# Pools that wait tile by tile on two stacks, and the ternary weights of layer 1 prepared inside layer 0

## The chip, the core and the metric

The kernel runs on one core of a Trainium2 chip. A core has five engines with queues of their own: TensorE (PE for its matmuls, PEld for its weight loads), VectorE (DVE), ScalarE (ACT), GpSimd (POOL) and SyncE (SP), which here only issues DMA transfers. Each engine works through its queue in order. Data lies in SBUF, 128 partitions wide, and the results of matmuls in PSUM, 8 banks of 2 KB per partition. The metric is the time of one execution in microseconds of device time; lower is better.

## The reference: four layers of cross-attention and feed-forward

x has 16 tiles of 128 tokens by 256 features. Each of four layers adds a cross-attention to the context of the same tile and then a feed-forward, each on a layer norm of x:

```
x = x + L0_xattn(norm(x), ctx)   # 16 heads, int8-rounded weights and activations
x = x + L0_ffn(norm(x))          # causal self-attention (16 query heads, rotary), then 8 experts
x = x + L1_xattn(norm(x), ctx, mask)
x = x + L1_ffn(norm(x))          # ternary weights
x = x + L2_xattn(norm(x), ctx)   # 16 heads
x = x + L2_ffn(norm(x))          # 64 low-rank routes, the best 4
x = x + L3_xattn(norm(x), ctx)   # every query against all 2048 context rows
x = x + L3_ffn(norm(x))          # 8 experts and 2 shared
```

The change touches the weights of L1_ffn, which the reference rounds so:

```
def weight_quant(w):
    scale = 1.0 / jnp.clip(jnp.mean(jnp.abs(w)), EPS, None)
    return jnp.clip(jnp.round(w * scale), -1.0, 1.0) / scale
gate = bit_linear(x, w_gate); up = bit_linear(x, w_up)
activated = subln(up * jnp.square(jax.nn.relu(gate)), subln_weight)
return bit_linear(activated, w_down)
```

Three matrices of 256 x 1024 are divided by their mean absolute value, rounded and cut to -1, 0, 1. Only layer 3 looks across tiles, and it does so through the context alone; layers 0 to 2 of a tile need nothing of another tile.

## The kernel before: three stages of pools and interleaved steps

The program has three stages: layer 0 (`l0`), layers 1 and 2 with the keys and values of layer 3 (`middle`), and layer 3 (`l3`). In each, the work on a tile is cut into generators that yield between steps. `side_by_side` (line 122) holds a table `starts` of step numbers, starts generators at their step and advances all running ones by one piece a step. In layer 0 tile t starts its cross-attention (`l0_xattn`) at step 4t, the keys of the self-attention (`l0_keys`) at 4t+8, its four groups of heads (`l0_group`) at 4t+11 to 4t+14, its experts (`l0_moe`) at 4t+17. In `middle` it starts `l1_xattn` at 4t, `l3_keys` at 4t+2, `l1_ffn` at 4t+3, `l2_xattn` at 4t+7, `l2_ffn` at 4t+16, and `l3_values` starts once at step 4.

The steps are only the order in which the program is written. The framework's scheduler then sets the order of each engine's queue, taking instructions as they get ready, the earlier written first, and adds the semaphores. In `l3` the order is fixed by hand (`manual_schedule`, line 1142).

A tile of SBUF or PSUM comes from a pool. A pool has a number of buffers for each tag and lies on a stack: a pool opened after another has been closed takes over its bytes. As written before, the first use of a new pool waits until the pools whose bytes it takes have been released as a whole. All pools lie on one stack (left). The streams have two pools each, one for tiles and one, `_s`, for small columns (`stream`, line 116).

The joint between the stages: `run` (line 1182) opens pool w0 with all weights of layer 0, closes it, opens w3 (weights of layer 3's attention and its keys `kst` and values `v_int`), and inside it `middle` opens w1 (weights of layers 1 and 2), the PSUM pool with tags e=1, w=3, x=2, av=1, f=1 bank, and calls `l1_ffn_weights` (line 612). That loads gate, up and down into a pool l1r (8 KB per partition each), sums their absolute values (line 622), adds the sums over the partitions with one matmul (line 624), and rounds: two passes on VectorE (lines 631, 632) and one on ScalarE, which writes bf16 (line 633). `load`, `rows` and `cols` (lines 91 to 113) each issue one DMA on SP. Then come the loads of `l2_xattn_weights`, `l2_ffn_weights` and `l3_kv_weights`, and with the first step those of `l1_xattn` for context and mask (lines 583, 585). Layer 0's PSUM pool has tags x, av, aq, a, as, ap with one bank each, and m with two; `l1_xattn` and `l1_ffn` work through tag e, `l3_keys` and `l3_values` and `l2_ffn` through tag f, `l1_ffn`'s gate and up and `l2_ffn`'s vecs through tag w.

Layer 3's first steps (lines 1146 to 1155): norm (965), transpose (971), projection (980), quantisation (987), transpose of q (1004), scores (916), then the exponentials on ScalarE (938). Each takes a bank from b0 to b6 in turn (`take`, line 904).

Of the kernel before, what the change touches and what calls it, by code (L numbers as in the profile page):

```python
# [4 lines left out]

# [1 line left out]

# [1 line left out]

# [9 lines left out]
F32 = mybir.dt.float32  # L19
BF16 = mybir.dt.bfloat16  # L20
# [5 lines left out]
ALU = mybir.AluOpType  # L26
AX = mybir.AxisListType
PSUM = bass.MemoryType.PSUM

P = 128  # L30
# [10 lines left out]
class Net:  # L41
# [66 lines left out]
    def cols(self, name, tag):  # L108
# [3 lines left out]
        self.nc.sync.dma_start(t, self.i[name].rearrange("(c p) -> p c", p=P))  # L112
        return t

    @contextmanager
    def stream(self, name, bufs=2, small=3, tag=None):

        with (self.tc.tile_pool(name=name, bufs=bufs) as pool,
              self.tc.tile_pool(name=f"{name}_s", bufs=small) as sm):
            yield pool, sm, tag or name  # L120

    def side_by_side(self, starts):
# [26 lines left out]
    @contextmanager  # L149
    def psum(self, **bufs):  # L150

        with self.tc.tile_pool(name="psum", bufs=1, space=PSUM) as self.ps:
            self.bufs = bufs
            yield
            self.ps = None
# [174 lines left out]

    def l0_xattn_weights(self):
        w = {}
        with self.tc.tile_pool(name="l0x_q", bufs=1) as pool:
            w["q"], w["sq"] = self.quant_weight("L0_xattn_wq", pool, "l0q")
            w["p"], w["sp"] = self.quant_weight("L0_xattn_wp", pool, "l0p")
        w["kv"] = self.load("L0_xattn_wkvT", [P, 2, 512], "x2", "(c p) o -> p c o", p=P)
        w["bq"], w["bp"] = self.rows("L0_xattn_bq", "b0"), self.rows("L0_xattn_bp", "b1")
        w["bv"] = self.rows("L0_xattn_bkv", "b2", slice(D, 2 * D))
        w["bk"] = self.cols("L0_xattn_bkv", "bc0")
        return w  # L340
# [102 lines left out]

    def l0_ffn_weights(self, pool):
        nc, w = self.nc, {}
        w["q"] = self.load("L0_ffn_qT", [P, 2, 2048], "wa", "(c p) n -> p c n", p=P)
        w["kv"] = self.load("L0_ffn_kvT", [P, 2, 1024], "wc", "(c p) n -> p c n", p=P)
# [12 lines left out]
        w["ct"], w["st"] = ct, st  # L460
        w["moe"] = self.moe_weights("L0_ffn", 8)
        return w

    def rotated(self, ps, w, j, pool):
# [88 lines left out]
        out = yield from self.moe(hT, w["moe"], 8, 1e-9, pool, 1)  # L553
        nc.vector.tensor_tensor(self.x[t], out, self.x[t], ALU.add)

    @contextmanager
    def l0_weights(self, pool):
        self.tag = "x"
        yield self.l0_xattn_weights(), self.l0_ffn_weights(pool)

    def l0(self):

        with self.tc.tile_pool(name="l0w", bufs=1) as wp, self.psum(x=1, av=1, aq=1, a=1, **{"as": 1}, ap=1, m=2), self.l0_weights(wp) as (wx, wf), (
                self.stream("x", bufs=1, small=2)) as sx, self.stream("a") as sa, self.stream("m", small=2) as sm:
            tiles = {}

            starts = {}
            for t in range(NT):
                starts.setdefault(4 * t, []).append((sx, lambda p, t=t: self.l0_xattn(t, wx, p)))
                starts.setdefault(4 * t + 8, []).append((sa, lambda p, t=t: self.l0_keys(t, wf, tiles, p)))  # L570
                for g in range(4):
                    starts.setdefault(4 * t + 11 + g, []).append(
                        (sa, lambda p, t=t, g=g: self.l0_group(t, g, wf, tiles, p)))
                starts.setdefault(4 * t + 17, []).append((sm, lambda p, t=t: self.l0_moe(t, wf, tiles, p)))
            self.side_by_side(starts)
        self.tag, self.small = None, self.small0


    def l1_xattn(self, t, pool):
# [32 lines left out]
    def l1_ffn_weights(self):  # L612

        nc, W = self.nc, self.W1
        w = {"subln": self.rows("L1_ffn_subln_weight", "subln")}
        with self.tc.tile_pool(name="l1r", bufs=1) as pool:
            raw = [self.load("L1_ffn_gateT", [P, 2, W], "ra", "(c p) n -> p c n", p=P, pool=pool),
                   self.load("L1_ffn_upT", [P, 2, W], "rb", "(c p) n -> p c n", p=P, pool=pool),
                   self.load("L1_ffn_downT", [P, 8, D], "rc", "(c p) n -> p c n", p=P, pool=pool)]
            sums = self.s(3, "wsum")  # L620
            for j, r in enumerate(raw):
                nc.vector.tensor_reduce(sums[:, j:j + 1], r, AX.XY, ALU.add, apply_absolute_value=True)
            ps = self.mm([P, 3], "wtot")
            nc.tensor.matmul(ps, self.ones, sums, start=True, stop=True)
            mean = w["mean"] = self.w.tile([P, 3], F32, name="wmean", tag="wmean")
            nc.vector.tensor_scalar(mean, ps, 1.0 / (W * D), 1e-5, ALU.mult, ALU.max)
            r = self.s(3, "wr")
            nc.vector.reciprocal(r, mean)
            for j, (n, v) in enumerate(zip(("gate", "up", "down"), raw)):
                w[n] = self.w.tile(list(v.shape), BF16, name=f"tern{j}", tag=f"tern{j}")  # L630
                nc.vector.tensor_scalar(v, v, r[:, j:j + 1], 1.0, ALU.mult, ALU.min)
                nc.vector.tensor_scalar(v, v, -1.0, MAGIC, ALU.max, ALU.add)
                nc.scalar.activation(w[n], v, AF.Identity, bias=self.unmagic)
        return w

    def l1_ffn(self, t, w, pool):

# [223 lines left out]

    def middle(self, w3):

        with (self.tc.tile_pool(name="w1", bufs=1) as self.w, self.psum(e=1, w=3, x=2, av=1, f=1)):
            self.tag = "e"
            w1f = self.l1_ffn_weights()
            w2x, w2f, w3k = self.l2_xattn_weights(), self.l2_ffn_weights(), self.l3_kv_weights()
            with (self.stream("f", bufs=1, small=2) as s2f, self.stream("x", bufs=1, small=2) as s2x,
                  self.stream("kv", bufs=1, small=2, tag="f") as s3, self.stream("f1", bufs=1, small=2, tag="e") as s1f,
                  self.stream("x1", bufs=1, small=2, tag="e") as s1x):  # L870
                starts = {}
                for t in range(NT):
                    for step, st, make in ((0, s1x, lambda p, t=t: self.l1_xattn(t, p)),
                                           (3, s1f, lambda p, t=t: self.l1_ffn(t, w1f, p)),
                                           (7, s2x, lambda p, t=t: self.l2_xattn(t, w2x, p)),
                                           (16, s2f, lambda p, t=t: self.l2_ffn(t, w2f, p)),
                                           (2, s3, lambda p, t=t: self.l3_keys(t, w3k, w3, p))):
                        starts.setdefault(4 * t + step, []).append((st, make))
                starts[4].append((s3, lambda p: self.l3_values(w3k, w3, p)))
                self.side_by_side(starts)  # L880
        self.tag, self.small = None, self.small0

    def l3(self, w3, moe_w):
# [10 lines left out]
        NE, IN = 10, 176  # L894
        LAG = 4
        E = mybir.EngineType
        with (tc.tile_pool(name="l3x", bufs=2) as pool, tc.tile_pool(name="l3p", bufs=3) as pp,
              tc.tile_pool(name="l3t", bufs=LAG + 1) as tp, tc.tile_pool(name="l3m", bufs=1) as mp,
              tc.tile_pool(name="l3e", bufs=3) as ep):
            st = {}  # L900

            banks = {f"b{j}": float(j - 7) for j in range(7)}
# [278 lines left out]

    def run(self):
        self.load_x()
        with self.tc.tile_pool(name="w0", bufs=1) as self.w:
            self.l0()
        with self.tc.tile_pool(name="w3", bufs=1) as self.w:
            w3 = self.l3_weights()
            self.middle(w3)
            with self.tc.tile_pool(name="w4", bufs=1) as self.w:
# [72 lines left out]
```

## Time and profile before

| | |
|---|---|
| median of 3 runs | 3008.33 us (3003.62 to 3014.27) |
| the profiled execution's own time | 3011.51 us |
| its span, first to last instruction | 3009.8 us |
| busy in the span | PE 2460.5 (82%), DVE 1956.3 (65%), ACT 1755.0 (58%), POOL 1000.7 (33%), PEld 1556.2 (52%) |
| last addition of layer 0 to x (line 554) | 1154.6 us after the start |
| last addition of layer 2 to x (line 770) | 1862.5 us |
| first exponential of layer 3 (line 938) | 1877.5 us |
| weights loaded by SP around the joint (8960 KB in 24 transfers) | issued 1121.9 to 1169.3 us |

The page cuts the span into 40 slices of 75 us and gives a digit of busy tenths for each; the granted clock of TensorE has a line of its own. Slices 0 to 14 are layer 0, 15 to 24 the middle, the rest layer 3:

```profile
PE   4789999999999875888888885777777777777778
...
ACT  1234444444444332555555541998888888888885
...
PEclk9899999999999887999999997589899898989999
DMA  5000000000000003000000002876666666666673
```

TensorE is at 9 through most of layer 0 and falls to 7 and 5 at its end; it is at 8 in the middle and falls to 5 at that one's end; in layer 3 ScalarE is the busiest. The DMA engines work at the beginning, in slice 15, and through layer 3.

### The profile page before, as it was taken

The page shows a single profiled execution, that of the slowest core. Times are in us where ns is not written, and L with a number is a line of the kernel's source. Part 1 is how long each engine was busy: PE and PEld are TensorE (multiplying, and loading weights), DVE is VectorE, ACT ScalarE, POOL GpSimd, SP SyncE. Part 2 cuts the span into 40 slices and gives each one's busy share as a digit, 9 for nine tenths or more (in the row PEclk, how much of TensorE's full clock was granted, in tenths as well). Part 3 has the DMA queues.
Part 4 walks back from the last instruction along what each step waited for, and adds up shares of the span by engine and source line. Part 5 has one row for each costly group of instructions (what it writes and reads, how often), then busy time and mean ns, then how long its engine had stood idle before and what let it go on. Part 6 is the DMA issues. An engine that isn't in the chain of part 4 may idle for free. (4 is left out here: it accounts for less than half of the span.)

```text
span 3009.8 us, 41685 instructions
## 1 busy us (share of the span) xinstructions
PE 2460.5 (82%) x14066; PEld 1556.2 (52%) x14066; DVE 1956.3 (65%) x5041; ACT 1755.0 (58%) x4636; POOL 1000.7 (33%) x1587
## 2 busy tenths in 40 slices
PE   4789999999999875888888885777777777777778
PEld 2456666666666543456555653344444444444445
DVE  2455666666665434566666653887788787878784
ACT  1234444444444332555555541998888888888885
POOL 2344444444443322555555541111111111112111
PEclk9899999999999887999999997589899898989999
DMA  5000000000000003000000002876666666666673
GB/s 205 1 1 1 1 1 1 1 1 1 1 1 1 1 28 102 6 3 5 5 5 4 3 1 72 154 135 123 124 117 128 121 124 121 126 122 125 118 128 62
DMA packets 559830, 171.38 MB, mean 57 GB/s; under 512 B 538912, under 2 KB 555904, under 8 KB 558848
## 3 DMA queue, kind: packets, MB, share of 16 engines
q1 hardware_dynamic: 559616, 168.72, 27.8%
q8 instruction: 111, 1.82, 0.2%
q14 instruction: 103, 0.84, 0.1%
HBM read 32.37 MB, written 2.10 MB: 11 GB/s over the span
## 5 line engine op out<-in xcount | busy, mean ns | idle before, releaser
L938 ACT ACTIVATE p<-piece,nb,hs 128x512 int16<-128x512 f32 x1024 | 785.2, 791 | 27.4 <-issue 17.0
L922 DVE TENSOR_REDUCE nm<-piece 128x1 f32<-128x512 f32 x1024 | 652.1, 684 | 107.7 <-PE piece L916 99.8
L916 PE MATMUL piece<-kst,qT 128*128 128x512 bf16 x1024 | 366.5, 414 | 200.6 <-DVE ma L1099 89.6
L1100 POOL TENSOR_TENSOR act<-ma,mb 128x176 f32<-128x176 f32 x160 | 89.0, 558 | 765.1 <-DVE ma L1099 764.7
L233 PE MATMUL gu<-w_L_ffn_wgu,mhT 128*128 128x352 f32 x640 | 252.5, 523 | 11.6 <-ACT p L938 8.0
L225 ACT COPY pT<-tp 128x512 f32<-128x512 f32 (+1 forms) x208 | 116.6, 563 | 201.6 <-PE tp L209 200.1
L916 PEld LDWEIGHTS <-qT 128*128 128x128 bf16 x1024 | 77.4, 99 | 297.2 <-issue 168.8
L938 ACT ACTIVATION_READ_ACCUMULATOR p<-piece,nb,hs 128x1 f32 x1024 | 222.2, 217 | 0.0
L259 POOL TENSOR_TENSOR kx<-kT,hmask 128x512 f32<-128x512 f32 x128 | 132.8, 1043 | 190.4 <-PE scores L262 125.4
L264 DVE TENSOR_REDUCE mx<-scores 128x4 f32<-128x512 f32 x128 | 88.2, 689 | 161.3 <-PE scores L262 161.0
L233 PEld LDWEIGHTS gu<-w_L_ffn_wgu,mhT 128*128 128x128 f32 x640 | 122.7, 205 | 131.4 <-ACT p L938 83.5
L950 PEld LDWEIGHTS <-pT 128*128 128x128 f16 x4096 | 144.7, 99 | 82.6 <-issue 68.0
L278 PEld LDWEIGHTS av<-v,pT 128*128 128x128 f32 x1024 | 136.2, 201 | 78.2 <-ACT pT L225 66.6
L233 PE MATMUL gu<-w_L_ffn_wgu,hT 128*128 128x352 f32 x512 | 173.7, 461 | 2.1 <-DVE act L432 1.6
L524 ACT ACTIVATE s<-s,nb,qs 128x128 f32<-128x128 f32 x256 | 123.2, 482 | 87.2 <-DVE nb L522 87.2
L278 PE MATMUL av<-v,pT 128*128 128x17 f32 x1024 | 136.3, 265 | 41.0 <-ACT pT L225 41.0
L269 ACT ACTIVATE p<-scores,mx,qs 128x128 f32<-128x128 f32 x256 | 96.9, 459 | 118.8 <-DVE mx L267 111.0
L950 PE MATMUL av<-v_int,pT 128*128 128x16 bf16 x4096 | 143.7, 171 | 19.6 <-DVE o L1021 19.6
L262 PE MATMUL scores<-kx,qT 128*128 128x512 f32 x256 | 153.0, 682 | 2.3 <-ACT qT L225 1.8
L539 PE MATMUL oproj<-w_L_ffn_oT,oT 128*128 128x256 f32 x512 | 128.9, 396 | 3.7 <-ACT oT L533 3.6
L1119 PE MATMUL moe<-w_L_ffn_wd,aT 128*128 128x256 f32 x448 | 127.7, 434 | 3.6 <-ACT p L938 3.6
L233 PE MATMUL q<-w_L_ffn_qT,hT 128*128 128x512 f32 x256 | 127.9, 600 | 2.1 <-DVE rot L478 2.0
(362 smaller groups left out, 5305.7 us busy)
## 6 DMA issues: line engine op xcount, KB each, us to landing
pT<-p SPq DMA_TRANSPOSE x256, 4.3
w_L_ffn_wgu<-in_L_ffn_wgu SPq DMA_DIRECT2D x1, 3520.0 KB, 11.6
w_L_ffn_wgu<-in_L_ffn_wgu SPq DMA_DIRECT2D x1, 2816.0 KB, 12.7
x<-in_x SPq DMA_DIRECT2D x16, 128.0 KB, 4.5
ctxT<-in_ctxT SPq DMA_DIRECT2D x4, 512.0 KB, 5.2
w_L_ffn_qT<-in_L_ffn_qT SPq DMA_DIRECT2D x1, 2048.0 KB, 7.9
w_L_ffn_oT<-in_L_ffn_oT SPq DMA_DIRECT2D x1, 2048.0 KB, 15.6
ctx<-in_ctx SPq DMA_DIRECT2D x16, 128.0 KB, 2.0
```

The costliest lines, as they stand in the source:

```text
L225: nc.scalar.copy(out[:, j0:j0 + m, :], ps)
L233: self.nc.tensor.matmul(ps, a, b, start=(j == 0), stop=(j == n - 1))
L259: nc.gpsimd.tensor_tensor(kx, kT[oc].unsqueeze(1).to_broadcast([P, 4, P]), self.hmask[:, hs].unsqueeze(2).to_broadcast([P, 4, P]), ALU.mult)
L262: nc.tensor.matmul(ps, qT[:, oc, :], kx, start=True, stop=True)
L278: nc.tensor.matmul(av[:, 4 * g + h, :], pT[:, h, :], v[:, 4 * g + h, :], start=True, stop=True)
L524: nc.scalar.activation(s[:, j, :], s[:, j, :], AF.Exp, bias=nb[:, j:j + 1], scale=qs[:, j:j + 1], accum_out=z[:, j:j + 1])
L539: nc.tensor.matmul(proj, oT[:, j, :], w["o"][:, c, :], start=(c == 0), stop=(c == 15))
L916: nc.tensor.matmul(ps, qTs[t % 2][:, hd, :], kst[q // 2][:, hd // 2, 512 * (q % 2):512 * (q % 2) + 512], start=True, stop=True)
L922: nc.vector.tensor_reduce(st["nm", u][:, q:q + 1], st["s", u, q][0], AX.X, ALU.max, negate=True)
L938: nc.scalar.activation(p[:, 512 * q:512 * q + 512], ps, AF.Exp, bias=nb, scale=st["sq", t][:, hd:hd + 1], accum_out=st["z", t][:, hd, q:q ...
L950: nc.tensor.matmul(st["av", t][:, hd, :], pb[:, c, :], v[:, c, hd * 16:(hd + 1) * 16], start=(c == 0), stop=(c == NT - 1))
L1119: nc.tensor.matmul(ps, st["aT", k][:r, j, :], wd[:r, c, :], start=(c == 0), stop=(c == 13))
```

## The change

Every pool except the two constant ones is opened with `reuse_waits="tile"`: a tile waits for those tiles alone whose bytes it takes over, not for their whole pool. The pools lie on two stacks: on the right layer 0's cross-attention (wx and stream x), later layer 1 (w1, x1, f1), later the experts of layer 3 (w4); on the left the rest. When layer 0's cross-attention has been written to its end, at step 68 of layer 0, a generator `prepare` closes its two pools, opens w1 in their place and runs `l1_ffn_weights` there, in pieces between the steps 68 to 71: load and round one matrix after the other through two raw buffers instead of three, each with its own sum, matmul (in bank x of layer 0), and mean. `middle` opens its streams in another order (x1 and f1 on the right; then w2, kv, x, f on the left). In `l0_ffn_weights` the load of keys and values comes before that of the queries, and the experts' weights have a pool of their own, wm.

```diff
+    def pool(self, name, bufs, side="left"):
+        return self.tc.tile_pool(name=name, bufs=bufs, side=side, reuse_waits="tile")
...
-        with self.tc.tile_pool(name="psum", bufs=1, space=PSUM) as self.ps:
+        with self.tc.tile_pool(name="psum", bufs=1, space=PSUM, reuse_waits="tile") as self.ps:
...
+    def l0(self, late):
+        early = ExitStack()
         self.tag = "x"
+        with self.psum(x=1, av=1, aq=1, a=1, **{"as": 1}, ap=1, m=2):
+            self.w = early.enter_context(self.pool("wx", 1, "right"))
+            wx = self.l0_xattn_weights()
+            sx = early.enter_context(self.stream("x", bufs=1, small=2, side="right"))
+            with (self.pool("wa", 1) as self.w, self.stream("a") as sa, self.pool("wm", 1) as wm,
+                  self.stream("m", small=2) as sm):
+                wf = self.l0_ffn_weights(self.w)
+                self.w = wm
+                wf["moe"] = self.moe_weights("L0_ffn", 8)
+                self.tiles(wx, wf, sx, sa, sm, early, late)
...
+        def prepare(pool):
+            early.close()
+            self.w = late.enter_context(self.pool("w1", 1, "right"))
+            yield from self.l1_ffn_weights()
+        starts.setdefault(4 * NT + 4, []).append((sa, prepare))
+        self.side_by_side(starts)
...
+        with self.pool("l1r", 1, "right") as pool:
+            raw = {n: self.load(f"L1_ffn_{n}T", shape, f"raw{j % 2}", "(c p) n -> p c n", p=P, pool=pool)
+                   for j, (n, shape) in enumerate(shapes.items()) if j < 2}
+            for j, (n, shape) in enumerate(shapes.items()):
+                yield
+                if j == 2:
+                    raw[n] = self.load(f"L1_ffn_{n}T", shape, "raw0", "(c p) n -> p c n", p=P, pool=pool)
+                v, total, r = raw[n], self.s(1, "wsum"), self.s(1, "wr")
+                nc.vector.tensor_reduce(total, v, AX.XY, ALU.add, apply_absolute_value=True)
+                ps = self.bank([P, 1], "x", "wtot")
+                nc.tensor.matmul(ps, self.ones, total, start=True, stop=True)
+                nc.vector.tensor_scalar(mean[:, j:j + 1], ps, 1.0 / (W * D), 1e-5, ALU.mult, ALU.max)
+                nc.vector.reciprocal(r, mean[:, j:j + 1])
+                nc.vector.tensor_scalar(v, v, r, 1.0, ALU.mult, ALU.min)
                 nc.vector.tensor_scalar(v, v, -1.0, MAGIC, ALU.max, ALU.add)
                 nc.scalar.activation(w[n], v, AF.Identity, bias=self.unmagic)
...
+        with (self.psum(e=1, w=3, x=2, av=1, f=1), self.stream("x1", bufs=1, small=2, tag="e", side="right") as s1x,
+              self.stream("f1", bufs=1, small=2, tag="e", side="right") as s1f, self.pool("w2", 1) as self.w,
+              self.stream("kv", bufs=1, small=2, tag="f") as s3, self.stream("x", bufs=1, small=2) as s2x,
+              self.stream("f", bufs=1, small=2) as s2f):
             w2x, w2f, w3k = self.l2_xattn_weights(), self.l2_ffn_weights(), self.l3_kv_weights()
...
     def run(self):
         self.load_x()
+        late = ExitStack()
+        self.l0(late)
+        with self.pool("w3", 1) as self.w:
             w3 = self.l3_weights()
             self.middle(w3)
+            late.close()
+            with self.pool("w4", 1, "right") as self.w:
                 moe_w = self.moe_weights("L3_ffn", 10)
```

The tables of starts are the same but for `prepare`, and the arithmetic on x is the same.

More of the change, by code (lines that the diff above doesn't have):

```diff
@@ L8 @@
-from contextlib import contextmanager
+from contextlib import ExitStack, contextmanager
 import numpy as np
@@ L113, in cols, with stream @@
         return t
+    def pool(self, name, bufs, side="left"):
+        return self.tc.tile_pool(name=name, bufs=bufs, side=side, reuse_waits="tile")
     @contextmanager
-    def stream(self, name, bufs=2, small=3, tag=None):
-        with (self.tc.tile_pool(name=name, bufs=bufs) as pool,
-              self.tc.tile_pool(name=f"{name}_s", bufs=small) as sm):
+    def stream(self, name, bufs=2, small=3, tag=None, side="left"):
+        with (self.pool(name, bufs, side) as pool,
+              self.pool(f"{name}_s", small, side) as sm):
             yield pool, sm, tag or name
@@ L332, in l0_xattn_weights @@
         w = {}
-        with self.tc.tile_pool(name="l0x_q", bufs=1) as pool:
+        with self.pool("l0x_q", bufs=1) as pool:
             w["q"], w["sq"] = self.quant_weight("L0_xattn_wq", pool, "l0q")
@@ L445, in l0_ffn_weights @@
         nc, w = self.nc, {}
+        w["kv"] = self.load("L0_ffn_kvT", [P, 2, 1024], "wc", "(c p) n -> p c n", p=P)
         w["q"] = self.load("L0_ffn_qT", [P, 2, 2048], "wa", "(c p) n -> p c n", p=P)
-        w["kv"] = self.load("L0_ffn_kvT", [P, 2, 1024], "wc", "(c p) n -> p c n", p=P)
         w["o"] = self.load("L0_ffn_oT", [P, 16, D], "wb", "(c p) n -> p c n", p=P)
@@ L460, in l0_ffn_weights @@
         w["ct"], w["st"] = ct, st
-        w["moe"] = self.moe_weights("L0_ffn", 8)
         return w
@@ L554, in l0_moe @@
         nc.vector.tensor_tensor(self.x[t], out, self.x[t], ALU.add)
-    @contextmanager
-    def l0_weights(self, pool):
+    def l0(self, late):
+        early = ExitStack()
         self.tag = "x"
[L559 to L575, printed above, removed]
-        self.tag, self.small = None, self.small0
@@ new lines, in l0, with tiles @@
+        self.tag, self.small = None, self.small0
+    def tiles(self, wx, wf, sx, sa, sm, early, late):
+        tiles = {}
+        starts = {}
+        for t in range(NT):
+            starts.setdefault(4 * t, []).append((sx, lambda p, t=t: self.l0_xattn(t, wx, p)))
+            starts.setdefault(4 * t + 8, []).append((sa, lambda p, t=t: self.l0_keys(t, wf, tiles, p)))
+            for g in range(4):
+                starts.setdefault(4 * t + 11 + g, []).append(
+                    (sa, lambda p, t=t, g=g: self.l0_group(t, g, wf, tiles, p)))
+            starts.setdefault(4 * t + 17, []).append((sm, lambda p, t=t: self.l0_moe(t, wf, tiles, p)))
+        def prepare(pool):
[4 more added lines that the diff above has]
+        self.side_by_side(starts)
@@ L614, in l1_ffn_weights @@
         nc, W = self.nc, self.W1
[L615 to L631, printed above, removed]
@@ new lines, in l1_ffn_weights @@
+        mean = self.w.tile([P, 3], F32, name="wmean", tag="wmean")
+        w = self.w1f = {"mean": mean, "subln": self.rows("L1_ffn_subln_weight", "subln")}
+        shapes = {"gate": [P, 2, W], "up": [P, 2, W], "down": [P, 8, D]}
+        for n, shape in shapes.items():
+            w[n] = self.w.tile(shape, BF16, name=f"tern_{n}", tag=f"tern_{n}")
+        with self.pool("l1r", 1, "right") as pool:
[12 more added lines that the diff above has]
+                nc.vector.tensor_scalar(v, v, r, 1.0, ALU.mult, ALU.min)
@@ L632, in l1_ffn_weights @@
                 nc.vector.tensor_scalar(v, v, -1.0, MAGIC, ALU.max, ALU.add)
                 nc.scalar.activation(w[n], v, AF.Identity, bias=self.unmagic)
-        return w
     def l1_ffn(self, t, w, pool):
@@ L862, in middle @@
     def middle(self, w3):
-        with (self.tc.tile_pool(name="w1", bufs=1) as self.w, self.psum(e=1, w=3, x=2, av=1, f=1)):
-            self.tag = "e"
-            w1f = self.l1_ffn_weights()
-            w2x, w2f, w3k = self.l2_xattn_weights(), self.l2_ffn_weights(), self.l3_kv_weights()
[L868 to L880, printed above, removed]
@@ new lines, in middle @@
+        self.tag = "e"
+        w1f = self.w1f
+        with (self.psum(e=1, w=3, x=2, av=1, f=1), self.stream("x1", bufs=1, small=2, tag="e", side="right") as s1x,
+              self.stream("f1", bufs=1, small=2, tag="e", side="right") as s1f, self.pool("w2", 1) as self.w,
+              self.stream("kv", bufs=1, small=2, tag="f") as s3, self.stream("x", bufs=1, small=2) as s2x,
+              self.stream("f", bufs=1, small=2) as s2f):
+            w2x, w2f, w3k = self.l2_xattn_weights(), self.l2_ffn_weights(), self.l3_kv_weights()
+            starts = {}
+            for t in range(NT):
+                for step, st, make in ((0, s1x, lambda p, t=t: self.l1_xattn(t, p)),
+                                       (3, s1f, lambda p, t=t: self.l1_ffn(t, w1f, p)),
+                                       (7, s2x, lambda p, t=t: self.l2_xattn(t, w2x, p)),
+                                       (16, s2f, lambda p, t=t: self.l2_ffn(t, w2f, p)),
+                                       (2, s3, lambda p, t=t: self.l3_keys(t, w3k, w3, p))):
+                    starts.setdefault(4 * t + step, []).append((st, make))
+            starts[4].append((s3, lambda p: self.l3_values(w3k, w3, p)))
+            self.side_by_side(starts)
@@ L896, in l3 @@
         E = mybir.EngineType
-        with (tc.tile_pool(name="l3x", bufs=2) as pool, tc.tile_pool(name="l3p", bufs=3) as pp,
-              tc.tile_pool(name="l3t", bufs=LAG + 1) as tp, tc.tile_pool(name="l3m", bufs=1) as mp,
-              tc.tile_pool(name="l3e", bufs=3) as ep):
+        with (self.pool("l3x", bufs=2) as pool, self.pool("l3p", bufs=3) as pp,
+              self.pool("l3t", bufs=LAG + 1) as tp, self.pool("l3m", bufs=1) as mp,
+              self.pool("l3e", bufs=3) as ep):
             st = {}
@@ L1183, in run @@
         self.load_x()
-        with self.tc.tile_pool(name="w0", bufs=1) as self.w:
-            self.l0()
-        with self.tc.tile_pool(name="w3", bufs=1) as self.w:
+        late = ExitStack()
+        self.l0(late)
+        with self.pool("w3", 1) as self.w:
             w3 = self.l3_weights()
             self.middle(w3)
-            with self.tc.tile_pool(name="w4", bufs=1) as self.w:
+            late.close()
+            with self.pool("w4", 1, "right") as self.w:
                 moe_w = self.moe_weights("L3_ffn", 10)
```

## The prediction, made before the result was known

> **What bounds the kernel now.** I read the table by windows first, over the joint between layer 0 and the layers 1 and 2 and over a steady stretch of the latter (columns: window, its length, then busy us and instruction count of PE, PEld, DVE, ACT, POOL, then the granted TensorE clock, DMA share, GB/s):
>
> ```profile
> 985.00:1060.00 75.00, 63.04 (x241) 39.47 (x239) 32.42 (x88) 29.39 (x82) 26.21 (x37) 0.89 0.00 1
> 1060.00:1110.00 50.00, 38.72 (x173) 27.14 (x173) 21.36 (x58) 18.33 (x57) 8.56 (x11) 0.95 0.00 1
> 1110.00:1155.00 45.00, 35.19 (x118) 23.71 (x118) 17.80 (x42) 6.71 (x18) 2.85 (x5) 0.79 0.20 70
> 1155.00:1205.00 50.00, 22.23 (x63) 10.40 (x63) 26.24 (x71) 15.37 (x26) 15.74 (x33) 0.69 0.42 131
> 1425.00:1650.00 225.00, 192.62 (x967) 132.81 (x966) 154.41 (x433) 120.47 (x306) 121.12 (x196) 0.95 0.02 5
> ```
>
> TensorE carries both stages: in the steady middle it is busy 192.62 of 225 us, 86%, and VectorE 69%. At the joint it is not: from 985 on the last tiles of layer 0 leave it 33 us idle in 170, and from 1155 to 1205 it works 22 of 50 us at clock 0.69. So time is to be had at the joint, by giving TensorE work earlier. The timeline says why there is none:
>
> ```profile
> 1154.62 0.37 SPq L95 DMA_DIRECT2D w_L_xattn_Wq<-in_L_xattn_Wq  x1
> 1154.63 0.42 DVE L554 TENSOR_TENSOR x<-moe,x 128x256 f32<-128x256 f32 x1 [5.11 <-PE moe L233]
> ...
> 1155.11 0.39 PE L624 MATMUL wtot<-wsum,ones 128*128 128x3 f32 x2 [0.52 <-DVE x L554]
> ```
>
> ```profile
> 1176.93 2.08 PE L233 MATMUL k<-w_L_xattn_Wkv,ctxT 128*128 128x256 f32 x4 [7.39 <-DMA w_L_xattn_Wkv<-in_L_xattn_Wkv]
> ...
> 1179.13 0.29 POOL L587 CAST m<-mask 128x128 f32<-128x128 uint8 x1 [6.20 <-DMA mask<-in_mask]
> ```
>
> The queue of SP issues nothing from 1122.8 until layer 0's last matmul has ended (1154.62), then 21 loads one behind the other, and after them the first ctx and mask, which is used at 1179.1. The weights' sum (line 624) waits for the last bank of layer 0, and the rounding follows it to 1166.7. None of this needs layer 0's last tiles: x of tile 0 was final at 286.7 (first run of line 554). The waits are the pools', not the data's. The rows of single lines give the pace (columns: count, duration min/median/max ns, first and last start):
>
> ```profile
> L608 DVE SCALAR_TENSOR_TENSOR x<-read,rz,x x16: 446/461/485, 1183.3 to 1736.7; 128x256 f32<-128x256 f32 x16
> L675 DVE SCALAR_TENSOR_TENSOR x<-down,cd,x x16: 472/478/487, 1210.9 to 1770.7; 128x256 f32<-128x256 f32 x16
> L717 DVE TENSOR_TENSOR x<-out,x x16: 424/425/426, 1269.9 to 1819.9; 128x256 f32<-128x256 f32 x16
> ```
>
> Layer 1's feed-forward ends tile 0 at 1210.9 and tile 15 at 1770.7: 37.3 us a tile.
>
> **What comes free when.** I laid out both stacks by hand from the tile shapes, in the order of the tile calls. Right: w1 (16 KB) and the raw buffers (16 KB) fall on the bytes of layer 0's cross-attention, whose last step ended at 960.9 (line 371). x1 and f1 fall on the raw buffers. PSUM in order of first use: e takes x's old bank, f takes av's, both idle after 960.9. So layer 1's weights can be loaded from about 961, rounded as VectorE finds room, and layer 1's attention and feed-forward can run from about 1000, among layer 0's last steps; only the banks w (on a, aq, as, in use to about 1115) narrow the feed-forward. Left: w3's four loads fall on kvT (last read 1020), w2 on the stream a (last read 1121). But kv, x and f, the streams of layer 3's keys and of layer 2, lie on the expert weights wgu and wd and on the stream m, read until 1147.0 and 1154.6. Layer 2 therefore can't start before layer 0 ends, though its weights will be there.
>
> **The sum, part by part.**
>
> Gap. With weights and masks in place, the 22.23 us that TensorE works in 1155 to 1205 at clock 0.69 are 22.23 x 0.69/0.95 = 16.1 us warm, and at the middle's density (0.856) take 18.9 us: 50 - 18.9 = **31 us less**.
>
> Fill. In the steady window the matmul groups of layer 1 (gate, up, down, its transposes, scores against ctxT, read) add up to 45.9 us for six tiles, 7.65 us a tile. The idle 33 us would hold 4.3 tiles. Their own chain, all through the one bank e, passed a tile each 30 us in the ramp (line 608: 1183.3, 1214.2, 1243.1 in the timeline), so five fit into 1000 to 1155, and layer 0's instructions go first. I take 3.5, between none and five: 3.5 x 7.65/0.856 = **31 us less** later on, since work done early leaves the TensorE-bound middle. Layer 2 then finds x of tile 0 ready at 1155, which before it had at 1211.
>
> Rounding moved. Per matrix one reduce of 2.28 us (line 622), 1.28 (line 631), 1.22 (line 632) on VectorE, 2.0 on ScalarE (line 633), a matmul and two small ones: 14.3 us on VectorE, which in 985 to 1060 is busy 43%. Its queue is in order, so what is behind a 2.28 us reduce waits: rot, scores, the experts' products of layer 0, for which TensorE waits. From 0 to 14.3 us; I take a third, **5 us more**. Three loads of 1 MB go past SP's queue, empty there. ScalarE's 6 us sit in a 39% busy engine.
>
> Here a rule speaks against the change. The Trainium skill, "SBUF — State Buffer", section "Who interferes with whom", says that a VectorE instruction in a two-port mode, tensor_scalar among them, and a GpSimd instruction block each other for their whole length, tensor_reduce never. The trace agrees:
>
> ```profile
> 1163.43 1.21 DVE L632 TENSOR_SCALAR w_L_ffn_downT<-w_L_ffn_downT 128x2048 f32<-128x2048 f32 x1
> 1163.57 1.48 POOL L178 TENSOR_TENSOR ln_r<-rp,mhalf 128x1 f32<-128x1 f32 x1
> ```
>
> That power takes 0.55 us elsewhere; it stood about 0.9 us. By the rule all six tensor_scalars, 7.5 us, could stand in GpSimd's way; GpSimd is busy 26.21 of 75 us there, so by these rows 0.35 x 7.5 = 2.6 us meet. It is inside my 5; by the rule alone the term would be up to 7.5 more.
>
> Interleaving. Layer 0's tail is a chain of short hops; each can meet a foreign matmul of 0.2 to 0.6 us. Some 35 hops x 0.3 = 10 us, against a clock that stays up: 35.19 x (1 - 0.79/0.95) = 6 us back. From 6 less to 15 more; I take **5 more**. As layer 2 hangs on layer 0's last bytes, this counts one to one.
>
> Start. The cross-attention's stream no longer stands above the rounding scratch; its first matmul, at 26.9 now, could use the bank from 22.4 on. From 0 to 4.5 less; **1 less**, since the ramp has slack behind it. kvT now lies on that scratch, so its load waits from 19.5 to about 26; first read at 86.5: nothing. That cover is 57 us; were it gone, 7 us.
>
> End. Layer 3's first steps wait for the pools of layer 2:
>
> ```profile
> 1862.54 0.42 DVE L770 TENSOR_TENSOR x<-out,x 128x256 f32<-128x256 f32 x1 [11.83 <-PE out L233]
> ...
> 1862.94 0.41 DVE L965 TENSOR_SCALAR ln_h<-x,ln_mv,ln_r 128x256 f32<-128x256 f32 x1
> ```
>
> Norm and transpose get free. The projection takes bank b1, which is f's, and f is read by line 770 until 1863.0. It started at 1864.45: **1.4 less**. If b1 were another bank, up to 14 (the first exponential is at 1877.5). The load of layer 3's experts comes earlier and was hidden.
>
> Sum: 31 + 31 - 5 - 5 + 1 + 1.4 = 54.4. From the span 3009.8 that is 2955.4; with the 1.7 us around it 2957.1 against this execution's 3011.5; the median shown is 3.2 lower: **2954 us**.
>
> **Rivals.**
> Only the gap closes (0.19): the scheduler or the queue of SP keeps layer 1 behind layer 0, say because masks stand behind w2's loads, which wait for 1121. For it: SP is in order, and the mask came last before. Against: the loads of gate, up and down went at 1121.9, before Wq, which is written earlier; loads go as they get ready. Layer 1 then starts near 1155 instead of 1179: 24 - 5 = 19 less, 2989.
> The pools still wait as a whole (0.05): no gain but order, 3008. Against: gate's load at 1121.9 came right after the last read in stream a, so waits follow bytes already at the grain of pools.
> The middle gets slower (0.14): layer 1 far ahead takes the three banks w from layer 2's vecs, two of which are held through the choice of routes, and the period grows. It has to grow from 37.3 by 54/15 = 3.6 us to eat the gain; at 5.5 us it is 15 x 5.5 - 54 = 28 more, 3036. For it: 86% busy, bufs=1 everywhere. Against: what is written later gets what is left over, and at the end, without layer 1, tiles pass in 24 to 31 us, so layer 2's own chain has room.
>
> **How the numbers follow.** The forecast has 0.62: with fill of 1.5 to 5 tiles, rounding 0 to 14, interleaving -6 to +15 it spans 2925 to 2985. The range adds the first rival: 2922 to 2996. A measurement of this kernel tells some 0.3%, 9 us, from no change. Faster 0.81, same 0.05, slower 0.14.
>
> **What would show it.** Right: tern activations before 1060; line 608's first run before 1100; line 717's first near 1210 and its last near 1765; PE above 85% in 1000 to 1155; DMA near zero after 1155; projection of line 980 right after line 770. Wrong: line 608 first after 1150 (first rival); 717's interval above 41 us (third); layer 0's last line 554 later than 1175.

## The result, and the profile after

The changed kernel takes 2978.28 us (median of 4 runs, 2974.05 to 2980.08) against 3006.93 us before (median of 4 runs): ratio 0.9898, 95% interval 0.9879 to 0.9917. The forecast was 2954, 54 us less; the gain is 28.65 us, inside the range (2922 to 2996), but just over half of what was summed.

The page of after, slices of 75 us in tenths (the lines shown of before):

```profile
PE   4789999999999877788888885777777777777778
...
PEclk9999999999999998999999996699998999999999
DMA  5000000000000011000000003876666666666662
```

The slice in which TensorE fell to 5 after layer 0 is gone; its clock stays at 8 or 9 there. The weights are issued from 957.0 to 1117.8 us, before layer 0 ends. But slices 13 to 15 stand at 8, 7, 7: layer 0's tail is as thin as it was. The table by windows says it in numbers (columns as in the prediction: window, length, busy us and count of PE, PEld, DVE, ACT, POOL, clock, DMA share, GB/s):

```profile
985.00:1060.00 75.00, 60.86 (x243) 37.92 (x241) 42.21 (x107) 31.14 (x85) 30.77 (x49) 0.93 0.06 18
1060.00:1110.00 50.00, 37.59 (x157) 24.94 (x157) 18.79 (x54) 17.92 (x55) 7.28 (x9) 0.90 0.15 42
1110.00:1150.00 40.00, 34.00 (x125) 24.22 (x125) 12.92 (x42) 6.50 (x18) 2.56 (x8) 0.82 0.25 80
1150.00:1200.00 50.00, 35.40 (x126) 17.62 (x126) 28.62 (x86) 23.00 (x53) 25.62 (x45) 0.86 0.03 7
1425.00:1650.00 225.00, 192.21 (x960) 133.05 (x966) 154.35 (x436) 120.72 (x310) 120.08 (x194) 0.95 0.02 5
```

From 985 to 1150 TensorE works 132.45 of 165 us; before, it was 132.36 us in the same stretch: nothing was filled. In the 50 us behind the joint it works 35.40 us where it was 22.23 (1155 to 1205). The steady middle is the same. The timeline of after shows what came early and what did not:

```profile
980.38 2.00 ACT L651 ACTIVATE tern_gate<-w_L_ffn_gateT,unmagic 128x2048 bf16<-128x2048 f32 x1 [1.04 <-DVE w_L_ffn_gateT L650]
...
985.68 0.42 SPq L601 DMA_DIRECT2D mask<-in_mask  x1
...
995.25 0.41 DVE L193 TENSOR_SCALAR ln_h<-x,ln_mv,ln_r 128x256 f32<-128x256 f32 x1 [0.51 <-POOL ln_r L182]
...
1143.15 5.01 PE L237 MATMUL moe<-w_L_ffn_wd,actT 128*128 128x256 f32 x22 [0.46 <-DVE actT L231]
...
1148.01 0.38 PE L213 MATMUL tp<-ident,ln_h 128*128 128x128 f32 x2
...
1152.74 0.47 DVE L624 SCALAR_TENSOR_TENSOR x<-read,rz,x 128x256 f32<-128x256 f32 x1
```

The first matrix is rounded at 980 and the last at 996, the masks are loaded from 986 on, and layer 1's first norm is done at 996, all as forecast. Its transpose needs nothing more: its bank was left at 990.6, when line 647 had read the last sum. Yet it runs at 1148.01, directly behind layer 0's last product. The row has no idle time and no releaser in brackets, so TensorE did not stand still for it; the transpose stood behind layer 0's products in TensorE's queue. Line 624 comes first at 1152.7, the sign named for "only the gap closes".

The table goes step by step. It uses a second profile of the changed kernel (span 2981.1 us, the experiment change_again), since the first profile ran ahead by chance in its first 200 us:

| step | forecast | measured |
|---|---|---|
| start (first run of line 546, 543 before) | -1 | +0.7 (200.2 against 199.5) |
| rounding in layer 0's last 190 us | +5 | +1.9 (965.9 to 1157.1 against 965.3 to 1154.6) |
| layer 1's tiles among them | +5 | 0, there were none |
| gap: layer 0's last addition to layer 1's first | -31 | -24.2 (4.5 against 28.7) |
| the ramp behind it, to layer 1's last addition | inside the gap | -5.1 (582.3 against 587.4) |
| fill | -31 | 0 |
| last addition of layer 2 to first exponential | -1.4 | -0.4 (14.6 against 15.0) |
| the rest of the middle and layer 3 | 0 | -1.5 |

The ramp is the time in which the second stage fills, tile by tile; its row runs on to layer 1's last addition, since the pace behind it is the same in both. The steps add up to -28.6; the spans differ by 28.7.

### The profile page after: what moved, and what is told of

It reads as the page before. It is cut to its first block, busy times and chain, and to the rows that moved or that the text cites. A ratio compares the mean times of both kernels' runs of the same rounds, so it can differ in the third digit from the quotient of the medians.

```text
span 2972.3 us, 41664 instructions
## 1 busy us (share of the span) xinstructions
PE 2438.9 (82%) x14053; PEld 1544.4 (52%) x14070; DVE 1958.2 (66%) x5045; ACT 1753.9 (59%) x4636; POOL 997.9 (34%) x1587
```

## The experiments

The question was why layer 1 did not run in layer 0's tail, and which part of the change brought the 29 us. **Order theory:** the framework's scheduler opens a pool, in the order that it writes, only after the pools whose bytes it takes have ended. Tile-wide waits change semaphores, not this order. All PSUM was one pool per stage, so no instruction of layer 1 that uses PSUM could be written before layer 0's last one. **Rivals:** the waits of single tiles brought the gain; or TensorE's queue was simply full of layer 0.

### pool_waits: the change without its waits

```diff
-        return self.tc.tile_pool(name=name, bufs=bufs, side=side, reuse_waits="tile")
+        return self.tc.tile_pool(name=name, bufs=bufs, side=side)
```

and the same in `psum`.

> The changed kernel with every pool back on pool-wide waits; two stacks and early rounding stay. The order of each engine's queue is the changed kernel's, instruction for instruction; only semaphore waits differ. Order theory (the gain came from the second stack and the earlier place of the rounding in the program, since the scheduler opens a pool in its order only after the pools whose bytes it takes): within 5 us of the changed kernel's 2978, so 2976 to 2984; first layer 1 x-addition (line 624) at 1152 to 1157, since the pool wait lets layer 1's first transposes start after the addition at 1148.2 instead of at 1147.8. Rival (the waits of single tiles brought the gain): near the kernel before, 2995 to 3007.

2990.43 us, ratio 0.9938 (0.9916 to 0.996): between the two. In the traces of pool_waits and change_again the instructions of every engine stand in the same order, so 12 us are the price of the waits alone. Layer 1's first addition comes 5.2 us behind layer 0's last (1158.1 to 1163.3), in change_again 4.5: the gap stays closed. The ramp took 8.5 more (590.8 against 582.3), and the joint to layer 3 5.7 more, which the timeline of pool_waits shows:

```profile
1845.91 0.42 DVE L787 TENSOR_TENSOR x<-out,x 128x256 f32<-128x256 f32 x1 [12.10 <-PE out L237]
1846.02 0.12 POOL L1160 MEMSET act<- 128x32 f32 x1 [10.12 <-PE out L237]
1846.09 3.55 POOL L1162 MEMSET qT<- 128x2048 bf16 x2
...
1849.97 0.56 POOL L182 TENSOR_TENSOR ln_r<-rp,mhalf 128x1 f32<-128x1 f32 x1
1850.57 0.41 DVE L982 TENSOR_SCALAR ln_h<-x,ln_mv,ln_r 128x256 f32<-128x256 f32 x1 [4.23 <-POOL ln_r L182]
```

GpSimd's memsets wait until layer 2's last product has ended (line 1160, 10.12 us idle); two of them take 3.55 us together, and the power for layer 3's first norm (line 182) stands behind them. In change_again these two ran at 1825.66, 10 us before the last addition. Of the ramp's 8.5 us, 7.6 arise between the tiles 1 and 8 of layer 1: against change_again its additions (line 692) are 2.6 us late at tile 1, 6.7 at tile 4, 9.2 at tile 5 and 10.2 from tile 8 on. Which waits make them is open.

### tile_waits_only: the waits without the rest

The kernel before with `reuse_waits="tile"` added to its pools, nothing else.

> The kernel before with tile-wide waits in every pool but the two constant ones, and nothing else of the change: one stack, layer 1's rounding at the head of the second stage. Order theory: no instruction changes its place in any queue; layer 1's masks stay behind the rounding, whose matmul stands behind layer 0's last bank. If the 12 us by which pool-wide waits slowed the changed kernel are a price of the waits themselves, this one gains a like sum, 993 to 1000 thousandths of the time before: 2990 to 3001. Rival (the waits of single tiles are worth something only with the second stack): within 4 us of before, 3002 to 3010.

2999.21 us, 0.9973 (0.996 to 0.9986). No engine's instructions changed their order between the traces of before and this run, as expected, and the waits gave 8 to 10 us (by the ratio and by the medians). The loads of SP in this run:

```profile
1120.45 0.37 SPq L95 DMA_DIRECT2D w_L_ffn_downT<-in_L_ffn_downT  x1
...
1147.64 0.38 SPq L95 DMA_DIRECT2D w_L_xattn_qT<-in_L_xattn_qT  x1
...
1161.63 0.43 SPq L585 DMA_DIRECT2D mask<-in_mask  x1
```

Before, layer 2's qT went at 1157.00 and the first mask at 1171.83. The mask is 10.2 us earlier, and layer 1's first addition comes at 1174.6 instead of 1183.3, while the rounding ends as late as before. So of the old gap the last 10 us were the masks behind SP's loads.

### late_rounding and rounding_left: the change without the early rounding

```diff
         def prepare(pool):
             early.close()
-            self.w = late.enter_context(self.pool("w1", 1, "right"))
-            yield from self.l1_ffn_weights()
+            self.w1 = late.enter_context(self.pool("w1", 1, "right"))
+            yield
```

with `l1_ffn_weights` run at the head of `middle`, after its PSUM pool is opened.

> The changed kernel with the generator that loads and rounds layer 1's weights written where it was before, at the head of the second stage (its pool is still on the right, on the bytes of the cross-attention, and waits tile by tile). Its loads and absolute sums need no PSUM and go early; its matmul for the sum over the partitions takes a bank of the second PSUM pool. Order theory: that matmul and the scaling behind it stand after 1148; gate's first matmul waits for it: 5 to 12 us more than the changed kernel, 2983 to 2990. Rival (loads and masks in time are all that counted, the rounding fits anywhere): within 3 us, 2975 to 2981.

3006.8 us, 0.9994 (0.9983 to 1.0005): all of the gain is gone, 28 us where 12 us was the most expected. My expectation counted the rounding's chain up to gate. The timeline shows a longer one:

```profile
1159.80 0.37 SPq L95 DMA_DIRECT2D w_L_ffn_downT<-in_L_ffn_downT  x1
...
1165.27 2.28 DVE L644 TENSOR_REDUCE wsum<-w_L_ffn_downT 128x1 f32<-128x2048 f32 x1
...
1173.18 1.22 DVE L650 TENSOR_SCALAR w_L_ffn_downT<-w_L_ffn_downT 128x2048 f32<-128x2048 f32 x1
...
1178.84 0.41 DVE L193 TENSOR_SCALAR ln_h<-x,ln_mv,ln_r 128x256 f32<-128x256 f32 x1 [0.48 <-POOL ln_r L182]
```

The first two scalings wait for sums from a bank of the new PSUM pool (layer 0 ended at 1153.4), the third matrix waits for a raw buffer, and the streams of layer 1 lie on the raw buffers, so that the first mask is issued at 1162.07 (985.68 in the changed kernel) and even the norm comes after the last scaling. In rounding_left the raw buffers lie on the left, under layer 2's weights:

```diff
-        with self.pool("l1r", 1, "right") as pool:
+        with self.pool("l1r", 1) as pool:
```

> The late rounding again, with its raw matrices on the left stack, on the bytes where layer 2's weights come afterwards, so that the streams of layer 1's steps (masks and context among them) no longer lie on the raw matrices. If the chain raw matrices, their bytes, masks, layer 1 is what cost the late rounding its 28 us, layer 1's first x-addition comes back to 1152 to 1158, only the feed-forward's gate waits for the rounding, and the time is 2982 to 2993. Rival (the rounding's own length on VectorE, the engine of layer 1's first steps, is what counts): first x-addition after 1170 and 2998 to 3010.

3003.21 us, 0.998 (0.9968 to 0.9992). Neither expectation held as a whole. Masks went at 963.8, layer 1's first addition came at 1167.1, 11.1 us behind layer 0's end instead of 36.3, but its time was lost again in another place:

```profile
1163.43 0.38 SPq L95 DMA_DIRECT2D w_L_ffn_downT<-in_L_ffn_downT  x1
...
1177.84 0.38 SPq L95 DMA_DIRECT2D w_L_xattn_qT<-in_L_xattn_qT  x1
...
1187.99 0.42 SPq L95 DMA_DIRECT2D w_L_xattn_Wkv<-in_L_xattn_Wkv  x1
```

Layer 2's and layer 3's weights now come behind the raw matrices. In both layouts something of the next stage lies on the late rounding's bytes and comes late. A layout in which nothing lies on them was not tried, so how much of the 28 us is the rounding itself and how much its bytes stays open.

### split_psum: two PSUM pools instead of one

```diff
-        with self.psum(x=1, av=1, aq=1, a=1, **{"as": 1}, ap=1, m=2):
+        with self.psum(aq=1, a=1, **{"as": 1}, ap=1, m=2):
+            early.enter_context(self.psum("right", x=1, av=1))
...
             early.close()
+            late.enter_context(self.psum("right", e=1, f=1))
```

`middle` then opens its own pool with w, x and av alone, and the sums of the rounding take bank e instead of x.

> The changed kernel with PSUM on two sides: layer 0's cross-attention has its two banks x and av in a pool of its own on the right, closed with it, and layer 1's e and f banks open there. Order theory: layer 1's first transpose stood behind layer 0's last matmul because the second PSUM pool is opened, in the scheduler's order, after the whole first one. With the split, layer 1's first x-addition (1152.7 in the changed kernel) comes before 1060; the feed-forward's gate, in bank w, still waits for layer 0's end but is ready then, at 1149 to 1155 instead of 1163. Some 8 to 14 us less than the changed kernel: 2964 to 2971. Rival (TensorE's queue is full of layer 0's instructions, which were written earlier and go first): first x-addition after 1145, time 2976 to 2981.

2980.43 us, 0.9916 (0.9896 to 0.9936). The order theory's first number came true, the full-queue rival's did not (timeline of split_psum):

```profile
1004.90 0.63 PE L213 MATMUL tp<-ident,ln_h 128*128 128x128 f32 x2
...
1038.72 0.59 PE L625 MATMUL read<-ctx,pT 128*128 128x256 f32 x2
...
1040.44 0.47 DVE L626 SCALAR_TENSOR_TENSOR x<-read,rz,x 128x256 f32<-128x256 f32 x1
```

Layer 1's first transposes (line 213) run at 1004.90 instead of 1148.01. In the trace of the changed kernel they are the matmuls directly behind layer 0's last product; in that of split_psum they stand 508 matmuls ahead of it. Nothing but the pools of PSUM was changed: this shows that the order of pools, not a full queue, kept layer 1 out.

The time did not follow. Tile 0's feed-forward ends at 1176.4; in the changed kernel, set to the same start, it ends at 1186 (first profile) or 1190 (second). This lead of 10 or 13 us has shrunk to 2 or 5 us at tile 2 and to 0 or 3.5 us at tile 15. Tile 0's gate, in bank w, starts at 1152.67, directly behind layer 0's last product, and tile 1's cross-attention ends only at 1178.4, behind tile 0's feed-forward in the one bank e.

### split_psum_ffn and keys_later: the feed-forward too, through bank f

```diff
-            gate, up = self.bank([P, 512], "w", "gate"), self.bank([P, 512], "w", "up")
+            tag = "f" if t < self.AHEAD else "w"
+            gate, up = self.bank([P, 512], tag, "gate"), self.bank([P, 512], tag, "up")
```

with AHEAD = 5, and layer 3's keys and values, the other users of f, 20 steps later.

> As the split of PSUM, and in addition the first five tiles of layer 1 take their gate and up products in bank f, while layer 3's keys and values, which used f from the first step on, start 20 steps later and follow every 3 steps. Order theory: one and a half to two tiles of layer 1 run to their end inside layer 0's tail (last of them near 1150); 2 x 7.65/0.856 = 18 us of the forecast's fill, 15 to 30 us less than the changed kernel: 2948 to 2963. Rival (full queue): 2976 to 2981. Rival (the interleaving costs layer 0's tail what it brings): layer 0's last x-addition (1148.2) moves to 1160 or later and the time stays above 2968.

2995.77 us, 0.9963 (0.9949 to 0.9976). Two tiles did end in or just behind layer 0's tail (1106.0 and 1158.5), and layer 0's end was not late (1155.5), but behind them the tiles of layer 1 came every 42 us on average instead of 37.4. So I took the shift alone:

> The changed kernel with the one other thing that the run through bank f had: layer 3's keys and values start 20 steps later and the keys follow every 3 steps. If this shift is why that run was slower (TensorE's work on the values, 16 products of 2.08 us each, leaves the ramp, where TensorE has room, for the steady part), the interval of layer 1's tiles goes above 40 us here too, and the time to 2990 to 3000. Rival (gate and up in one bank made it slow): within 5 us of the changed kernel, 2974 to 2984.

3020.67 us, 1.0041 (1.0025 to 1.0057), and 38 to 49 us between layer 1's tiles from tile 5 on. The shift is the cause, and costs more than expected: 42 us. In 1425 to 1650 TensorE works less than in the changed kernel, 186.50 against 192.96 us, on work of which more is left; TensorE waits at several new places there, of which the second row is the largest (us in total, times, longest):

```profile
PE av L282 <- ACT pT L229: 8.9, 7, 3.7
PE htp L806 <- DVE parts L841: 8.1, 2, 6.3
```

The second is not in the changed kernel's list, where the first stands with 18.3. A transpose of layer 3's keys comes up in TensorE's queue up to 6.3 us before its data is there. More work in the steady part and a worse order there both fit this; how much each costs was not separated.

### split_psum_e, split_psum_e2: through bank e, keys where they were

The same diff with `"e"` in place of `"f"` and AHEAD = 3, later 2; steps of keys and values as in the change.

> The split of PSUM, with the gate and up products of the first three tiles of layer 1 through bank e, and layer 3's keys and values at the steps of the changed kernel. Fill theory (work of layer 1 done in layer 0's tail leaves the second stage): two tiles end before 1165 as they did with bank f, and the pace behind is the changed kernel's 37.4 us a tile; so the second stage ends 15 to 35 us earlier: 2945 to 2965. Rival (the ramp takes the head start back, as it did with the split alone, since layer 2 and not layer 1 sets its length): 2972 to 2984, with the last x-addition of layer 1 near 1735.

2960.75 us, 0.985 (0.9827 to 0.9874): the fill is there.

> The split of PSUM with gate and up through bank e for two tiles only, those that fit into layer 0's tail; the third, which took 58 us from its cross-attention to its end through the one bank e, takes banks w, which are free by then. If that third tile held up the ramp, it ends near 1195 instead of 1220, and the time is 5 to 15 us less than with three: 2946 to 2956. Rival (layer 2 sets the length of the ramp): within 4 us of it, 2957 to 2965.

2951.14 us, 0.9814 (0.9797 to 0.983), the best of all and 27 us less than the changed kernel (2977.76 in the same round). Windows of split_psum_e2, then of change_again:

```profile
985.00:1150.00 165.00, 139.68 (x591) 93.51 (x591) 89.72 (x263) 69.00 (x189) 52.83 (x88) 0.92 0.16 44
1150.00:1200.00 50.00, 43.18 (x167) 24.04 (x165) 26.33 (x74) 24.93 (x61) 30.08 (x48) 0.93 0.01 4
```

```profile
985.00:1150.00 165.00, 133.61 (x511) 86.44 (x509) 76.39 (x202) 59.05 (x160) 40.83 (x65) 0.88 0.14 42
1150.00:1200.00 50.00, 36.14 (x139) 20.42 (x140) 25.27 (x79) 16.42 (x37) 18.03 (x33) 0.86 0.03 7
```

TensorE does 6 us more in the tail and, brought to clock 0.95, (43.18 x 0.93 - 36.14 x 0.86)/0.95 = 9.6 us more behind the joint. There layer 2 has two finished tiles to start on: its first addition (line 737 here, 734 in the changed kernel) comes at 1212.6 against 1249.0, 32 us earlier when set to the same start. Layer 0's tail is not slower for it: from the end of its twelfth tile to its last it takes 188.7 us (961.5 to 1150.2), and 187.9 and 191.2 in the two profiles of the change. The gain of two tiles over three was expected from the third tile ending near 1195; it ended at 1217.6, as before (1220.2). The time came out as expected, the reason did not; which part of the difference of the two medians is the spread between executions stays open.

### Putting layer 1 ahead

```diff
+            with self.tc.high_priority():
+                next(gen)
```

around each step of layer 1's first four tiles; in split_psum_e2_ahead `high_priority(300)` for two tiles.

> The split of PSUM with gate and up of four tiles through bank e, and the steps of layer 1's first four tiles put ahead of everything else in the scheduler's order, so that four tiles, not two, stand inside layer 0's tail. Fill theory: each further tile saves up to 7.65/0.856 = 9 us behind; layer 0's end moves later by what the foreign instructions cost its chain (the interleaving, forecast at 5 us for 3.5 tiles): 2940 to 2955. Rival (layer 0's chain pays for what is put ahead of it): its last x-addition comes more than 15 us later than in the split with two tiles (1153.3), and the time is 2960 or more.

2991.72 us, 0.9937 (0.9914 to 0.9961). Runs of layer 0's and layer 1's last additions (columns: duration min/median/max ns, first and last start):

```profile
L569 DVE TENSOR_TENSOR x<-moe,x x16: 387/425/426, 288.1 to 1193.6; 128x256 f32<-128x256 f32 x16
```

```profile
L707 DVE SCALAR_TENSOR_TENSOR x<-down,cd,x x16: 472/478/484, 1038.0 to 1754.8; 128x256 f32<-128x256 f32 x16
```

Four tiles of layer 1 end by 1121, and layer 0's end moves from 1153.3 (split_psum_e, in which two tiles ran early) to 1193.6: 38 us when set to the same start.

> The split of PSUM with gate and up of two tiles through bank e, and these two tiles moved up in the scheduler's order by 300 places only, so that they stand ahead of layer 0's last groups and experts but behind what was written before those. Fill theory: the two tiles end 20 to 40 us earlier than 1155.6, layer 0's end moves by less than 8 us (four tiles put ahead of everything moved it by 38), and a third tile's cross-attention and feed-forward start before layer 0's end: 2938 to 2950. Rival (layer 0's chain of short hops is what any foreign instruction delays, and layer 2 hangs on its end): layer 0's last x-addition 10 us later or more and 2954 or more.

2969.65 us, 0.9873 (0.9857 to 0.989): two tiles end by 1096.5, 64 us earlier than in split_psum_e2 at the same start, and layer 0's last addition is at 1173.3, 18 us later at the same start (288.2 and 283.0 are the first runs of that line). The rival holds in both runs: what is put ahead of layer 0 delays its end, and of the 27 us that two tiles brought in what was left over, 8 us remain.

### change_again

> The changed kernel itself, for a second profile of it. In its first profile layer 0 ran 4.8 us ahead of before from its first tile on (line 546: 194.7 against 199.5), and six kernels with the same beginning had 197 to 201. If the 4.8 us are a step of the change (the start), they are here again, 194 to 196; if they are the chance of one execution, the first run of line 546 is at 197 to 201. The time 2974 to 2984 in both cases.

2977.76 us, 0.9895 (0.9876 to 0.9913), and the first run of line 546 at 200.2: the 4.8 us of the first profile were one execution's chance.

## Why the prediction was half right

That the measured time lies inside the range is in part luck. A step worth 31 us did not happen at all, and two costs of 5 us each, set against it, came to 1.9 us and to nothing.

**The gap** (31 forecast, 29.3 measured with the ramp behind it) was read rightly from the window and its clock. The division among causes was not made in the forecast; the runs make it. Tile-wide waits alone give 8 to 10 us (tile_waits_only); the second stack and the early rounding with pool-wide waits 15 to 19 (pool_waits); the stacks and tile-wide waits without the early rounding nothing (late_rounding). So on two stacks, in both layouts tried, nothing or little was left of the gain without the early place of the rounding, and the 21 loads on SP that the forecast stressed were only the last 10 us of the gap.

**The fill** (31 forecast, 0 measured) is the step that failed, at the sentence "both idle after 960.9 ... layer 1's attention and feed-forward can run from about 1000". The bank was free and the data there. But a free bank in another pool is not a free bank to the scheduler: it wrote the first instruction of the second PSUM pool behind the last release of the first, whatever the waits allowed (1148.01; 1004.90 with the split). The banks w, which lay in such a pool too, did not open at "about 1115": even with the split, gate started at 1152.67, behind layer 0's last product. I had weighed this case as the first rival (19 less, 2989) and set it back because gate's load went before Wq's: an argument about SP's queue and SBUF's pools, which I carried over to PSUM, where one pool holds all. That rival named the scheduler or the queue of SP; it was the scheduler, and its example, masks behind w2's loads, was wrong: the masks were issued at 985.68.

**The size of the fill** was not too large per tile. With the split and bank e two tiles ran early and brought 27 us, where the forecast's 8.9 a tile make 18. The runs do not separate the rest; the earlier start of layer 2, which the forecast named but did not count, goes the right way. The 3.5 tiles were too many in what was tried: left to the scheduler, two fitted, and the runs that put four, or two, ahead paid 38 and 18 us at layer 0's end. With gate and up in a bank of their own (f) it was two as well; a third bank was not tried.

**Interleaving** (5 forecast for 3.5 tiles): nothing measurable for two tiles that take what is left over, and above the bound of 15 when put ahead (18 and 38). The estimate by hops fails for tiles put ahead.

**Rounding** (5 forecast, bounds 0 to 14.3): 1.9 in one profile, -1.4 in the other. TensorE was busy 24.29 of the 25 us from 960 to 985 in the first profile, in which two of the three matrices are rounded, and 24.32 before: the rounding did not make it wait there. But one tile did pay: the addition of line 546 for the fourteenth tile comes 62.9 and 63.1 us after the thirteenth's. It is 60.4 us in the kernel before, and 59.8 and 60.4 in late_rounding and rounding_left, which do not scale early. Some of these 2.6 us was made up again by layer 0's end in one profile, and more than all of it in the other. The port lock of the Trainium skill ("SBUF — State Buffer", "Who interferes with whom"), which the forecast took at 2.6 us, showed twice, here in the first profile: line 650 took 1.58 us instead of 1.22 beside line 482 on GpSimd, which it overlapped by 0.50, and line 649 took 1.42 instead of 1.29 beside line 530, overlapped by 0.34. Together 0.5 us, a fifth of my share. It is in kind as the page has it, though both delays are shorter than the overlap, where the page has the later one blocked until the first ends.

**Start** and **end** (1 and 1.4 less forecast): the start is not to be told from nothing, and the end gave 0.4. Layer 3's first norm still runs directly behind layer 2's last addition on VectorE (1835.98 and 1835.64 in change_again), as before.

**The middle gets slower** did not happen to the change (37.4 us a tile), but did to the two kernels that moved layer 3's keys and values out of the ramp.

## What to carry to other kernels

When a wait is relaxed, ask two questions: is the data there, and where does the instruction stand in its engine's queue. With this scheduler, a stage opened with one pool for all of PSUM stays a barrier in the order even when no semaphore holds it; give the banks that end early a pool of their own. Work put into another stage's idle time should come behind that stage's own chain. Here two tiles in what was left over brought 27 us; put ahead, they brought 8, and four put ahead cost 14.

## What was not expected of the hardware

The same program did not take the same time for its first 200 us in two executions. The rows are the same product in the first profile of the change and in the second:

```profile
95.71 1.02 PE L237 MATMUL v<-w_L_ffn_kvT,hT 128*128 128x512 f32 x2
```

```profile
96.99 1.91 PE L237 MATMUL v<-w_L_ffn_kvT,hT 128*128 128x512 f32 x2
```

From 90 to 120 us the granted clock was 0.95 in the first and 0.82 in the second, and TensorE took 20.56 us for 100 matmuls against 24.64 us for 96. Layer 0 was 5.5 us apart at its first tile (line 546: 194.7 and 200.2) and still 5.6 us at the end of its twelfth (960.3 and 965.9). Why the clock differed, the runs do not show. A difference of spans of two single profiles has to be read from a common starting point.
